# Step 2 of a graph layer: logits behind the group's products, ScalarE's search ahead of their exponentials (slots 1 and 3)

## The chip, the cores and the metric

The kernel runs on one core of one Trainium2 chip. The core has five engines, each with its own queue of instructions, and a wait in a queue holds what stands behind it:

- TensorE (PE in the profile; its weight loads are PEld) multiplies matrices and transposes tiles, out of SBUF into PSUM;
- VectorE (DVE) and ScalarE (ACT) do elementwise work, reductions and exponentials;
- GpSimd (POOL) does elementwise work here and starts the indirect DMAs (gathers);
- SyncE (SP) starts the other DMAs.

The metric is the time of one execution on the device in microseconds. Before the change it was 1398.09 us, the median of three runs (1396.92 to 1398.52).

## What is computed

Two layers over a graph of 2708 nodes with 256 features. Layer 0 is one sparse product, a projection, ReLU and a layer norm. Layer 1 makes two steps of attention that keeps only the largest probabilities of each row up to a mass of 0.9 ("top-p"), beside two products with the normalised graph matrix R. The part that matters here:

```
def _top_p_attention(X, W1, W2, W3):
    q = X @ W1.T @ W2.T
    k = X @ W3.T
    probs = softmax(q @ k.T, axis=-1)
    # keep the largest probabilities of each row until their sum reaches 0.9
    A = probs * mask
    return A / max(A.sum(-1), 1e-12)

for n in range(2):                       # STEPS
    A = _top_p_attention(Xa, W1, W2, W3)
    Xf = R @ Xf
    Xa = A @ Xa
    Z = Z + Xf @ U1[n].T + Xa @ U2[n].T
h = X + Z
out = layernorm(h)                       # then a residual and one more layer norm
```

## The kernel before

**Tiles.** The 2708 rows form NB = 22 blocks of 128 rows (the last has 20). A block of attention is a tile of 128 rows by 2708 columns in SBUF, called e. There are four (e0 to e3), taken in turn; `e2(t)` names the one of block t in step 2. Ahead of step 2 run layer 0, the lists of nonzero chunks of R, and step 1 of the attention. Step 2 starts some 800 us into the span.

**Periods.** Step 2 is the loop `for per in range(NB + 1)` (line 1128). In each period four blocks are in work at once, each one stage further than the next:

- `b_exp`, block per + 2: its logits are computed and exponentiated into e (`logits`, L506; `exps2`, L818, L821 and L822);
- `b_act`, block per + 1: ScalarE searches for the threshold in two rounds (`try_act`): a relu pass over the whole row (L922), a sign pass over the whole row (L925), and steps on single columns (L928, L930, and L935 to L938 in `next_level`);
- `b_dve`, block per: VectorE makes the exact cut (`last_level`, then the generator `finish2`: L976, maxima L979, sorting L576 and L578, marking L1007, and L1010, which writes the masked e);
- `t_mul`, block per - 1: PE transposes e in groups of four 128-column pieces (`turn`: transposes L526 into tr, ScalarE copies tr to wT at L529 and L532) and multiplies the pieces with ya (`products`, L563).

Beside these run the products with R (`r_units`, L730), fed by gathers on GpSimd (`y_load`, L698) and loads on SP, and the layer norms of finished rows (`final_slot`, L1037 to L1077), which need ScalarE's square root and four activations L1047 per period from period 13 on.

**Slots.** A period has NG = 6 slots, one for each group of `turn`. The order is written out by hand: whatever the loop emits first comes first on each engine's queue. `products(1)` in slot g multiplies the group of slot g - 1, so that ScalarE has a slot's time for the copy. The logits of a block come in three parts of 1024, 1024 and 660 columns. Part 0 of the next period's block is emitted in slot 5, and its maximum is taken by VectorE in slot 0 (`shift`, L815) as the shift of the exponentials. Part 1 is computed in slot 1, part 2 in slot 3. The exponentials of the parts are emitted in slots 0, 1 and 3; part 0 has a second one (L822). VectorE sums them in slot 5 (`begin_search`, L826 to L829).

**Buffers.** In PSUM[...] the logits tile `lg` takes two banks and exists once; tr, acc and misc have two of one bank each. So every logits product waits until ScalarE has read the tile for the part before. wT exists twice.

The order inside slots 1 and 3 before, on the queues concerned: PE does the transposes of the group, then (slot 1) the R products and the logits, or (slot 3) the logits and the R products, then the products of the group before. ScalarE does the copy to wT, the exponential of that part, then the search (in both slots: sign pass and small steps).

Of the kernel before, what the change touches and what calls it, by code (L numbers as in the profile page):

```python
# [148 lines left out]
def fast_path(ctx, tc, c, flags, fint, xT_d, x_d, w0_d, b0_d, w1_d, w2_d, w3_d, u1_d, u2_d, g_d, b_d):  # L149
# [13 lines left out]
    def ps_lg():  # L163
        return ps.tile([P, 2, CH], FP, tag="lg", name="lg", bufs=1)
# [4 lines left out]
    def ps_acc(t=None):  # L169
        acc = ps.tile([P, CH], FP, tag="acc", name="acc")  # L170
        if t == NB - 1:
            nc.vector.memset(acc[:, :D + 1], 0.0)
        return acc
# [121 lines left out]
    class Lists:  # L295
# [11 lines left out]
        def turn(self):  # L307
            n = self.n
            parts = names[:, self.a:self.b, :].rearrange("p m (s j) -> p (m s) j", j=3)
            tr = ps_tr()  # L310
            for j in range(3):
                nc.tensor.transpose(tr[:n, j, :], parts[:, :, j], ident)
            nc.scalar.copy(self.row[:n].rearrange("q (j p) -> q j p", j=3), tr[:n, :3, :])
# [184 lines left out]
    def logits(s, t, i):  # L498


        p = rows(t)
        lg = ps_lg()
        cs = CHS[2 * i:2 * i + 2]
        for h, (a, b) in enumerate(cs):
            o = slice(DA * h, DA * h + DA)
            nc.tensor.matmul(lg[:p, h, :b - a], lhsT=q[o, t * P:t * P + p], rhs=keys[s][o, i, :b - a],  # L506
                             start=True, stop=True)
        a, b = cs[0][0], cs[-1][1]
        return lg.rearrange("p h n -> p (h n)")[:p, :b - a], a, b
# [25 lines left out]
    def edge_product(y, acc, e):  # L535

        p = rows(EDGE)
        tr = ps_tr().rearrange("p k i -> p (k i)")[:, :NB * p].rearrange("p (k i) -> p k i", i=p)
        wT = work.tile([P, 4, P], FP, tag="wT", name="wT")
        wT = wT.rearrange("p k i -> p (k i)")[:, :NB * p].rearrange("p (k i) -> p k i", i=p)  # L540
        for k in [NB - 1] + list(range(NB - 1)):
            kw = rows(k)
            nc.tensor.transpose(tr[:kw, k, :], e[:p, k * P:k * P + kw], ident[:p, :p])
        for a, b, kw in ((0, NB - 1, P), (NB - 1, NB, rows(NB - 1))):
            nc.scalar.copy(wT[:kw, a:b, :], tr[:kw, a:b, :])
        for k in range(NB):
            kw = rows(k)
            o = EW * (k % 4)
            nc.tensor.matmul(acc[o:o + p, :D], lhsT=wT[:kw, k, :], rhs=y[:kw, k, :],
                             start=k < 4, stop=k >= NB - 4)  # L550

    def products(keep):

        if len(before) > keep:
            p, ks, wT, y, acc = before.pop(0)
            for k in ks:
                kw = rows(k)
                if p < P:
                    o = EW * (k % 4)
                    nc.tensor.matmul(acc[o:o + p, :D], lhsT=wT[:kw, k % 4, :p], rhs=y[:kw, k, :],  # L560
                                     start=k < 4, stop=k >= NB - 4)
                    continue
                nc.tensor.matmul(acc[:p, :D], lhsT=wT[:kw, k % 4, :p], rhs=y[:kw, k, :],  # L563
                                 start=k == 0, stop=k == NB - 1)
# [153 lines left out]
    def r_units(n):  # L718
        for _ in range(n):
            s, m = r_queue[0]  # L720
            p = rows(m)
            if not r_now:
                r_now[:] = [ps_misc(), 0]
                if m + 1 < NB:
                    r_load(s, m + 1)
            acc, k = r_now
            a, y = r_in[s, m]
            kw = CW if k < CC else p
            rhs = v[:p, m, :] if s and k == CC else y[:kw, k, :]
            nc.tensor.matmul(acc[:p, :D], lhsT=a[:kw, k, :p], rhs=rhs, start=k == 0, stop=k == CC)  # L730
            r_now[1] += 1
            if k == CC:
                r_now.clear()
                r_queue.pop(0)
                r_in.pop((s, m))
                base = za_load(m) if s else None
                later[1].append(lambda s=s, m=m, acc=acc, base=base: r_out(s, m, acc, base))
# [44 lines left out]
    def e2(t):  # L782
        return es[(t + 2) % 4]
# [30 lines left out]
    def shift(b, lg):  # L814
        nc.vector.tensor_reduce(b.nmax, lg[:, :P], AX.X, ALU.max, negate=True)  # L815

    def exps2(b, i, lg, a, c_):
        nc.scalar.activation(e2(b.t)[:b.p, a:c_], lg, AF.Exp, bias=b.nmax, scale=1.0,  # L818
                             accum_out=b.all[:b.p, i:i + 1])
        if i == 0:  # L820
            nc.scalar.activation(b.half, b.nmax, AF.Identity, bias=part_of[:b.p], scale=0.5)  # L821
            nc.scalar.activation(e2(b.t)[:b.p, HC:2 * HC], lg, AF.Exp, bias=b.half, scale=0.5, accum_out=b.roots)  # L822
# [41 lines left out]
    for t in range(NB):  # L864
# [6 lines left out]
        for g in range(NG):  # L871
# [5 lines left out]
            if b and g in (0, 2):  # L877
                lg = logits(1, b.t, g // 2)
# [38 lines left out]
    def try_act(b, k, part):  # L917


        e = e2(b.t)[:b.p, :N]  # L920
        if part == 0:
            nc.scalar.activation(scr[:b.p, :N], e, AF.Relu, bias=b.nz, scale=b.l[k], accum_out=b.relu)  # L922
            return
        if part == 1:
            nc.scalar.activation(scr[:b.p, :N], e, AF.Sign, bias=b.nz, scale=b.l[k], accum_out=b.sign)  # L925
            return
        if part == 2:
            nc.scalar.activation(b.n, b.sign, AF.Identity, bias=halfn[:b.p], scale=0.5)  # L928
            return
        nc.scalar.activation(b.u[k], b.relu, AF.Identity, bias=b.n, scale=b.rz)  # L930
        next_level(b, k)

    def next_level(b, k):
        keep, slope, down = STEPS[k]
        nc.scalar.activation(b.kept, b.l[k], AF.Copy, scale=keep + TOP_P * slope, bias=-down)  # L935
        nc.scalar.activation((b.l1, b.l2)[k], b.u[k], AF.Identity, bias=b.kept, scale=-slope)
        if k:
            nc.scalar.activation(b.few, b.l1, AF.Copy, scale=TOP_P, bias=-FEW)  # L938
# [185 lines left out]
    lg = logits(1, 3, 0)  # L1124
# [3 lines left out]
    for per in range(NB + 1):  # L1128
        if per == NB:
            tail.append(True)  # L1130
        n_r = units.get(per, 0)
        b_act = blocks.get(per + 1)
        b_dve = blocks.get(per)
        t_mul = per - 1 if per else None
        if per:
            accs[t_mul] = ps_acc(t_mul)
        masks = None
        b_exp = None
        if per and per + 2 < NB:
            b_exp = blocks[per + 2] = Block(per + 2)  # L1140
        for g in range(NG):
            n = n_r * (g + 1) // NG - n_r * g // NG
            now = later.pop(0)
            later.append([])
            if g == 0:
                if b_exp:
                    shift(b_exp, lg[0])
                r_units(n)
            if t_mul == EDGE:
                if g == 0:  # L1150
                    products(0)
                    edge_product(ya, accs[EDGE], e2(EDGE))
            elif per:
                turn(t_mul, g, ya, accs[t_mul], e2(t_mul))
            if b_exp and g == 3:
                lg = logits(1, b_exp.t, 2)
            if g == NG - 1 and 3 < per + 3 < NB:
                lg = logits(1, per + 3, 0)
            if g:
                r_units(n)  # L1160
            if b_exp and g == 1:
                lg = logits(1, b_exp.t, 1)
            if t_mul != EDGE:
                products(1 if per else 0)
            if b_exp and g in (0, 1, 3):
                exps2(b_exp, (g + 1) // 2, *lg)
            if b_act:
                for k, part in {0: ((0, 0),), 1: ((0, 1), (0, 2), (0, 3)), 2: ((1, 0),), 3: ((1, 1), (1, 2), (1, 3))}.get(g, ()):
                    try_act(b_act, k, part)
            if g == 0:  # L1170
                if b_dve:
                    last_level(b_dve)
                    masks = finish2(b_dve)
                    next(masks)
                final_slot(0)
                if per > 1:

                    t = t_mul - 1
                    base = za_load(t)
                    later[0].append(lambda t=t, base=base: arrive(t, base, accs.pop(t), ras.pop(t)[:rows(t)]))  # L1180
            elif masks:
                next(masks, None)
                if b_exp and g == 5:
                    begin_search(b_exp)
            for f in now:
                f()
            if g and (per < NB or g < NG - 1):
                final_slot(g)
# [407 lines left out]
```

## Time and profile before

| what | value |
|---|---|
| median of three runs | 1398.09 us |
| the profiled execution: its time, its span | 1400.2 us, 1398.4 us |
| mean granted TensorE clock in it | 0.965 |
| PE busy (matmuls) | 1280.4 us, 92% of the span |
| DVE busy | 1047.2 us, 75% |
| ACT busy | 742.1 us, 53% |
| POOL busy | 639.9 us, 46% |
| starts of L976, one a period, 0 to 21 | 805.16 to 1351.39 us |

Times of instructions are microseconds from the start of the span. A period is counted from one start of L976 to the next. The shares of busy time are means over the whole kernel; layer 0, step 1 and step 2 lean on different engines, so what holds for step 2 must be read from its own stretch. Matmuls are pipelined and the ends of their records are modelled, so that PE's busy time is not PE at its peak.

### The profile page before, as it was taken

The page shows a single profiled execution, that of the slowest core. Times are in us where ns is not written, and L with a number is a line of the kernel's source. Part 1 is how long each engine was busy: PE and PEld are TensorE (multiplying, and loading weights), DVE is VectorE, ACT ScalarE, POOL GpSimd, SP SyncE. Part 2 cuts the span into 40 slices and gives each one's busy share as a digit, 9 for nine tenths or more (in the row PEclk, how much of TensorE's full clock was granted, in tenths as well). Part 3 has the DMA queues.
Part 4 walks back from the last instruction along what each step waited for, and adds up shares of the span by engine and source line. Part 5 has one row for each costly group of instructions (what it writes and reads, how often), then busy time and mean ns, then how long its engine had stood idle before and what let it go on. Part 6 is the DMA issues. An engine that isn't in the chain of part 4 may idle for free.

```text
span 1398.4 us, 18915 instructions
## 1 busy us (share of the span) xinstructions
PE 1280.4 (92%) x5788; PEld 896.5 (64%) x5788; DVE 1047.2 (75%) x3488; ACT 742.1 (53%) x1336; POOL 639.9 (46%) x591
## 2 busy tenths in 40 slices
PE   8999999988999999999998948999998999798884
PEld 6877877833566666666666436777665666566662
DVE  2544545865888887776751279999999989999997
ACT  1000000025455555555554338888787888899950
POOL 1000000013554533775554276777733757767870
PEclk9999999999999999999999779999999999999997
DMA  6544544512222110232123244445432444445441
GB/s 182 179 152 152 164 146 155 162 34 66 65 93 67 50 55 9 88 100 69 58 67 91 71 144 142 145 147 158 147 109 84 132 161 126 132 129 169 136 144 38
DMA packets 92829, 157.93 MB, mean 113 GB/s; under 512 B 16356, under 2 KB 65196, under 8 KB 92720
## 3 DMA queue, kind: packets, MB, share of 16 engines
q1 hardware_dynamic: 66434, 100.59, 22.5%
q0 software_dynamic: 20544, 51.17, 13.0%
q10 hardware_dynamic: 5742, 4.89, 1.2%
q8 instruction: 48, 0.79, 0.2%
q14 instruction: 61, 0.50, 0.1%
HBM read 125.33 MB, written 31.26 MB: 112 GB/s over the span
## 4 chain that ended last, share of the span: by engine, by line
PE 55%; DVE 33%; ACT 5%; issue 2%; another core or an unknown queue 2%; DMA 2%; POOL 0%; ACTq 0%; DVEq 0%; POOLq 0%
PE acc L563 17%; PE acc L255 15%; PE lg L506 6%; DVE cand L979 5%; DVE w L1007 5%; PE tr L526 4%; DVE e L1010 4%; DVE w L976 4%; PE misc L677 3%; DVE srt L576 3%; DVE spare L578 3%; PE acc L649 2%; PE misc L427 2%; PE acc L461 2%
## 5 line engine op out<-in xcount | busy, mean ns | idle before, releaser
L529 ACT COPY wT<-tr 128x512 f32<-128x512 f32 (+2 forms) x258 | 132.3, 518 | 240.1 <-PE tr L526 145.3
L563 PE MATMUL acc<-ya,wT 128*128 128x256 f32 (+1 forms) x924 | 234.3, 393 | 13.4 <-ACT wT L529 8.2
L563 PE MATMUL acc<-x,wT 128*128 128x256 f32 (+1 forms) x924 | 232.8, 391 | 6.0 <-ACT wT L529 5.9
L698 POOL DMA_INDIRECT yg<-yf_d,ix x154 | 191.6, 1244 | 101.7 <-PE misc L730 51.2
L698 POOL DMA_INDIRECT yg<-v_d,ix x154 | 192.6, 1250 | 86.2 <-PE tr L526 38.7
L563 PEld LDWEIGHTS acc<-x,wT 128*128 128x128 f32 (+1 forms) x924 | 166.2, 191 | 87.8 <-issue 50.4
L563 PEld LDWEIGHTS acc<-ya,wT 128*128 128x128 f32 (+1 forms) x924 | 171.1, 193 | 70.1 <-issue 25.1
L255 PE MATMUL acc<-y,adj_t 128*128 128x257 f32 (+1 forms) x924 | 208.8, 382 | 0.0
L365 POOL DMA_INDIRECT adj_t<-in_adj,ix x154 | 170.9, 1110 | 51.0 <-issue 39.6
L255 PEld LDWEIGHTS acc<-y,adj_t 128*128 128x128 f32 (+1 forms) x924 | 171.5, 189 | 34.0 <-issue 10.3
L730 PE MATMUL misc<-yg,adj_t 128*128 128x256 f32 (+1 forms) x660 | 174.5, 398 | 11.8 <-DVE v L753 5.7
L506 PE MATMUL lg<-k,q 64*128 64x512 f32 (+3 forms) x528 | 154.6, 609 | 31.4 <-ACT e L822 28.6
L526 PE MATMUL tr<-ident,e 128*128 128x128 f32 (+2 forms) x946 | 148.4, 276 | 17.7 <-DVE e L1010 17.7
L730 PEld LDWEIGHTS misc<-yg,adj_t 128*128 128x128 f32 (+1 forms) x660 | 118.9, 193 | 59.1 <-issue 20.9
L526 PEld LDWEIGHTS tr<-ident,e 128*128 128x128 f32 (+2 forms) x946 | 113.5, 140 | 60.1 <-issue 16.7
L332 POOL DMA_DIRECT2D part_d<-e x1 | 0.6, 576 | 294.9 <-DVE e L331 294.9
L569 DVE MAX8 cand<-e 128x8 f32<-128x170 f32 (+1 forms) x352 | 88.1, 320 | 39.9 <-ACT e L513 22.4
L922 ACT ACTIVATE w<-e,st 128x2708 f32<-128x2708 f32 (+1 forms) x43 | 113.5, 2640 | 0.0
L925 ACT ACTIVATE w<-e,st 128x2708 f32<-128x2708 f32 (+1 forms) x42 | 111.0, 2642 | 0.1
L438 ACT COPY x1T<-tr 128x256 f32<-128x256 f32 (+1 forms) x22 | 8.0, 364 | 192.2 <-PE tr L437 192.2
L979 DVE MAX8 cand<-w 128x8 f32<-128x136 f32 (+1 forms) x440 | 93.5, 285 | 0.8
L576 DVE MAX8 srt<-spare 128x8 f32<-128x128 f32 (+3 forms) x264 | 81.4, 308 | 9.1
(230 smaller groups left out, 1794.0 us busy)
## 6 DMA issues: line engine op xcount, KB each, us to landing
adj_t<-in_adj SPq DMA_DIRECT2D x44, 704.0 KB
adj_t<-adjc_d SPq DMA_DIRECT2D x44, 448.0 KB
adjc_d<-adj_t SPq DMA_DIRECT2D x22, 256.0 KB
base<-za_d SPq DMA_DIRECT2D x41, 128.0 KB
adjc_d<-adj_t SPq DMA_DIRECT2D x22, 192.0 KB
xt<-in_x ACTq DMA_DIRECT2D x21, 128.0 KB
x_d<-x SPq DMA_DIRECT2D x21, 128.0 KB
x1b_d<-xb SPq DMA_DIRECT2D x21, 128.0 KB
```

What stands on the lines that cost most here:

```text
L255: nc.tensor.matmul(acc[:p, :n], lhsT=halves[k // KH][:kw, k % KH, :p], rhs=y[:kw, k, :n], start=k == 0, stop=stop and k == NB - 1)
L365: nc.gpsimd.indirect_dma_start(out=a[:CW, i, :], out_offset=None, in_=adj_rows, in_offset=bass.IndirectOffsetOnAxis(ap=ix[:CW, m, i:i + 1] ...
L506: nc.tensor.matmul(lg[:p, h, :b - a], lhsT=q[o, t * P:t * P + p], rhs=keys[s][o, i, :b - a], start=True, stop=True)
L526: nc.tensor.transpose(tr[:kw, k % 4, :p], e[:p, k * P:k * P + kw], ident[:p, :p])
L529: nc.scalar.copy(wT[:, :full, :p], tr[:, :full, :p])
L563: nc.tensor.matmul(acc[:p, :D], lhsT=wT[:kw, k % 4, :p], rhs=y[:kw, k, :], start=k == 0, stop=k == NB - 1)
L576: nc.vector.max(dst[:p, i:i + 8], src[:p])
L698: nc.gpsimd.indirect_dma_start(out=y[:CW, i, :], out_offset=None, in_=rows_d, in_offset=bass.IndirectOffsetOnAxis(ap=ix[:CW, m, i:i + 1], ...
L730: nc.tensor.matmul(acc[:p, :D], lhsT=a[:kw, k, :p], rhs=rhs, start=k == 0, stop=k == CC)
L922: nc.scalar.activation(scr[:b.p, :N], e, AF.Relu, bias=b.nz, scale=b.l[k], accum_out=b.relu)
L925: nc.scalar.activation(scr[:b.p, :N], e, AF.Sign, bias=b.nz, scale=b.l[k], accum_out=b.sign)
L979: nc.vector.max(cand[:p, 8 * i:8 * i + 8], w[:p, SEG2 * i:SEG2 * (i + 1)])
```

## The change

In slots 1 and 3 of the periods that have a block to exponentiate (`b_exp`, periods 1 to 19) the call of `logits` moves behind `products`, and the call of `exps2` moves behind the calls of `try_act`. In slot 0 the exponentials of part 0 stay where they were, ahead of the relu pass. In slot 5 nothing changes.

```diff
             elif per:
                 turn(t_mul, g, ya, accs[t_mul], e2(t_mul))
-            if b_exp and g == 3:
-                lg = logits(1, b_exp.t, 2)
             if g == NG - 1 and 3 < per + 3 < NB:
                 lg = logits(1, per + 3, 0)
             if g:
                 r_units(n)
-            if b_exp and g == 1:
-                lg = logits(1, b_exp.t, 1)
             if t_mul != EDGE:
                 products(1 if per else 0)
-            if b_exp and g in (0, 1, 3):
-                exps2(b_exp, (g + 1) // 2, *lg)
+            if b_exp and g in (1, 3):
+                lg = logits(1, b_exp.t, (g + 1) // 2)
+            if b_exp and g == 0:
+                exps2(b_exp, 0, *lg)
             if b_act:
                 for k, part in {0: ((0, 0),), 1: ((0, 1), (0, 2), (0, 3)), 2: ((1, 0),), 3: ((1, 1), (1, 2), (1, 3))}.get(g, ()):
                     try_act(b_act, k, part)
+            if b_exp and g in (1, 3):
+                exps2(b_exp, (g + 1) // 2, *lg)
             if g == 0:
                 if b_dve:
                     last_level(b_dve)
```

## The prediction

> **What bounds the kernel now.** I read the page first, for the span and the busy shares, then the busy time stretch by stretch, then the timelines of TensorE (PE), ScalarE (ACT) and VectorE (DVE) inside single periods of step 2. The change lies wholly in step 2, which takes the last 590 us.
>
> ```profile
> span 1398.4 us, 18915 instructions
> DVE  2544545865888887776751279999999989999997
> core 0: us, PE busy (x) PEld busy (x) DVE busy (x) ACT busy (x) POOL busy (x), PEclk, DMA share, GB/s
> 985.50:1010.00 24.50, 23.22 (x113) 17.11 (x112) 23.48 (x80) 19.97 (x34) 18.48 (x15) 1.00 0.49 150
> 1162.50:1189.30 26.80, 23.95 (x113) 16.92 (x111) 25.62 (x90) 24.21 (x40) 21.40 (x18) 1.00 0.47 148
> ```
>
> Each stretch is one period, from one start of L976 to the next. DVE is busy 23.48 of 24.5 us, the rest being small gaps between its own instructions, so it sets the pace. But PE has 23.22 us and, in the periods that also finish output rows (13 to 19), ACT has 24.21 of 26.8. Nobody is far behind. Such an engine can be pushed over the edge by a wait alone, so I looked at who waits for whom around the tile of the logits. It exists once, so each product into it waits for ScalarE's last exponential out of it. PE, period 7:
>
> ```profile
> 987.48 1.13 PE L506 MATMUL lg<-k,q 64*128 64x512 f32 x4 [0.32 <-ACT e L822]
> 988.53 1.99 PE L563 MATMUL acc<-ya,wT 128*128 128x256 f32 x8
> ...
> 1001.88 1.13 PE L506 MATMUL lg<-k,q 64*128 64x512 f32 x4
> 1002.93 1.56 PE L730 MATMUL misc<-yg,adj_t 128*128 128x256 f32 x6
> 1004.33 1.89 PE L563 MATMUL acc<-ya,wT 128*128 128x256 f32 x8
> 1006.06 1.03 PE L730 MATMUL misc<-yg,adj_t 128*128 128x256 f32 x4
> 1008.05 0.63 PE L526 MATMUL tr<-ident,e 128*128 128x128 f32 x4 [0.96 <-DVE e L1010]
> ```
>
> Columns: start, length, instruction, and in brackets the idle time before it and what ended it. PE loses 0.32 us before the logits of slot 1; before those of slot 5 (1001.88, for the next block) nothing. It then waits 0.96 us for DVE's L1010 before the next period's first transpose. That 0.96 us is PE's whole slack. ACT, same period:
>
> ```profile
> 984.31 0.59 ACT L529 COPY wT<-tr 128x512 f32<-128x512 f32 x1 [4.16 <-issue]
> ...
> 998.43 0.57 ACT L529 COPY wT<-tr 128x512 f32<-128x512 f32 x1
> 998.90 0.81 ACT L818 ACTIVATE e<-lg,nmax 128x660 f32<-128x660 f32 x1
> 999.60 0.20 ACT L818 ACTIVATION_READ_ACCUMULATOR e<-lg,nmax 128x1 f32 x1
> 999.70 2.64 ACT L925 ACTIVATE w<-e,st 128x2708 f32<-128x2708 f32 x1
> ...
> 1003.50 0.19 ACT L938 ACTIVATE st<-st 128x1 f32<-128x1 f32 x1
> 1003.60 0.73 ACT L529 COPY wT<-tr 128x512 f32<-128x512 f32 x2
> ```
>
> From 984.31 to 1003.60 ACT has no gap. The third exponential (L818, 660 columns, slot 3) ends at 999.71, over 2 us before PE wants the tile at 1001.88. Behind it stands the search: the sign pass L925 and the scalar steps L928 to L938, to 1003.60.
>
> **What the Trainium skill says.** "PSUM — Partial Sum Buffer", section "Engine vs sequencer instructions": the queues of ScalarE, VectorE and GpSimd are strict FIFO, and matmuls start and complete in program order. The trace agrees: in slot 1, PE's products stand idle behind the waiting logits. So a blocked logits product holds all of PE. "Perfetto Trace Analysis", section "Optimization Strategy": the same gap repeating on the engine that should be saturated can mean too few buffers; the 0.32 us gap in period after period, released by the tile's reader, is that. "TensorE: Matmul & The Clock Gate", Part 1, says PE drops to half clock after an idle window of about 3.4 us. Here, behind an idle time of 5.45 us, the logits at 1224.70 took 2.08 us instead of 1.13; this enters a rival.
>
> **The change, part by part.** No instruction is added or removed, no DMA moves; two orders change. One period (numbers of period 7):
>
> 1. PE, slot 1: the products of group 0 pass ahead of the logits. Their wT was copied at 984.31, so they start at once; the logits then come 1.9 us later, past the 0.32 us wait. Gain on PE 0.32 us (1.7 us in periods 14 and 17 to 19, where the table load of 1.28 us delays the exponentials). But next, in slot 2, PE needs ACT's copy of group 1, whose time has not moved: PE has 1.6 us to spare there in period 7, while in period 14 it already waits 0.27 us, so the gain becomes a longer wait. I count 0.
>
> 2. ACT, slot 1: sign pass and scalar steps (3.8 us) ahead of the second exponential, 1.1 us. The next copy comes when it came before. The slot 3 logits are the next to want the tile; the exponential now ends at 995.4 and they stand behind products that wait for that copy (995.32 to 995.9) and last 1.9 us. Cost 0.
>
> 3. PE, slot 3: products first, logits 1.06 us later. The third exponential starts at 1002.8 at the earliest (next point), so it is covered. Cost 0.
>
> 4. ACT, slot 3: the third exponential moves behind the sign pass and steps, from 998.90 to 1002.80, and ends at 1003.61. PE's slot 5 logits follow it: with the 0.15 us that the trace shows from the end of L822 (962.86) to the logits (963.01), they start at 1003.76, not 1001.88. That is **1.88 us later, against 0.96 us of slack**. This is the step that decides. Behind the waiting logits stand, on PE, the R products of slot 5, the products of group 4, those R products of slot 0 and the next first transpose.
>
> So a closed loop appears: ACT's first copy to the end of the third exponential, 1003.61 - 984.31 = 19.3 us; release 0.15; slot 5 logits to the next first transpose when nothing else holds it, 5.05 us (859.59 to 864.64 in period 1); transpose to copy 0.7 us (864.64 to 865.33). Sum **25.2 us**, against DVE's 24.46. In periods 14 to 18 the copy-to-copy part is 22.6 us (1161.29 to 1183.93 in period 14), because of the table load and four norm activations (L1047) in slot 0; loop 28.5 us against DVE's 26.8. Period 13: 21.6 us, loop 27.5. Period 10 has no R products, which fill 1.4 us of that stretch in slot 5 (1002.93 to 1004.33): 23.8.
>
> **When does DVE feel it?** DVE's shift (L815) reads slot 5's logits, and begin_search reads the third exponential. Period 1 shows the shift waiting:
>
> ```profile
> 860.77 0.29 DVE L815 TENSOR_REDUCE nmax<-lg 128x1 f32<-128x128 f32 x1 [0.82 <-PE lg L506]
> ```
>
> There L976 follows at 862.23 and ACT's first copy at 865.33. So L976 can't start earlier than 3.1 us before that copy. In the undisturbed periods the copy is 1.2 us ahead of L976, so the loop may fall 4.3 us behind before DVE pays. Adding up from the copy at 865.1 in period 2: eight loops of 25.2 to period 10 (1066.7), 23.8 to 11 (1090.5), two of 25.2 or 25.3 (1141.0), 27.5 (1168.5), five of 28.5: period 19 at 1311.0. Less 3.1, L976 of period 19 at 1307.9, where it was 1298.82: 9.1 us. By period 10 it is 4.5 us (1063.6 against 1059.14). Some 2.4 us that DVE already loses in periods 15 to 17 (28.54, 27.01 and 27.25 us, against 26.8) are within this sum. Period 19's begin_search could add 1 us. The tail doesn't touch the logits and keeps its length. I take **+9 us**: 1409.2 for a profiled execution, whose time before was 1400.2 (span 1398.4); the median shown, 1398.09, is 2.1 lower, so **1407**. An error of 0.15 us in the loop is 2.6 us over 17 periods: 1402 to 1411 is this case's own range.
>
> **Rivals.**
> - PE at half clock: in the final periods PE stands some 2.6 us before slot 5's logits (period 14: group 3's copy ends at 1179.34, its products and a transpose take 2.0 us, the exponential ends at 1183.93). Should this bring half clock for the 5 us stretch behind it, up to 5 us are added each time, right on the loop. Against: PE stands less elsewhere. Two such periods give 1415; chance 0.18.
> - The other side, not slower: DVE's slack swallows it. Ends of matmuls are modelled, so the 5.05 us stretch may be shorter. With 4.3 us or less the loop is 24.45 us, the light periods lose nothing, and five final ones lose 0.95 each, 4.7 us, about the 4.3 us that the slack takes. It decides from a loop of 24.5 us. 1398.5; chance 0.12. Against: 5.05 us is seen with PE working without a gap.
> - Faster: PE's 1.7 us in slot 1 of the final periods feed R products and gathers sooner and end the 2.4 us of DVE losses: 1395.5; chance 0.07. Against: ACT's copies don't move.
> - The orders come out as before in effect, because something else releases the tile: 1398; chance 0.05.
>
> **How the numbers follow.** The forecast has 0.58. Range 1398.5 to 1414: it takes in the upper part of the second rival and most of the first. 0.2% is 2.8 us, about what a measurement of this kernel tells from no change. Slower 0.58 + 0.18 + 0.02 of the second rival = 0.78; same 0.05 + 0.09 of it = 0.14; faster 0.07 + 0.01 = 0.08.
>
> **What would show it.** Right: PE's idle time before the logits passes from L822 to the third exponential, L818, about 1.2 us in the light periods (PE reaches slot 5 earlier by what it no longer loses) and over 2 in the final ones; no wait on L1010; DVE waiting before L815; L976 starts 25.2 and 28.5 us apart. Wrong: L976 still 24.46 us apart with PE waiting for L1010; or half-clock stretches on PE in the final periods.

## The result, and the profile after the change

The changed kernel takes **1415.51 us** (median of four runs, 1413.86 to 1417.31) against 1398.3 us for the kernel before, run beside it (four runs, 1396.92 to 1405.27). The ratio is 1.0124, with a 95% interval of 1.0099 to 1.015. It is slower, as forecast, but by 17 us where 9 were forecast.

The profiled execution took 1417.31 us. First its page: the span, the row of VectorE's busy tenths, and of the chain that ended last its shares by engine.

```profile
span 1415.5 us, 18896 instructions
...
DVE  2554545876888877767741569999997999989996
...
PE 66%; ACT 21%; DVE 9%; issue 2%; another core or an unknown queue 1%; DMA 0%; POOL 0%; ACTq 0%; DVEq 0%; POOLq 0%
```

The same line of the kernel before:

```profile
PE 55%; DVE 33%; ACT 5%; issue 2%; another core or an unknown queue 2%; DMA 2%; POOL 0%; ACTq 0%; DVEq 0%; POOLq 0%
```

This is the shortest sign that the bound has changed. Before, a third of the chain ran over VectorE. Now it has 9%, and the share has gone to PE and ACT. The busy times have hardly moved (PE 1284.0 us against 1280.4, DVE 1049.4 against 1047.2): no engine got more work, so the time went into waits.

Now single periods (each from one start of L976 to the next): period 8, the undisturbed pace of the light periods, then periods 10, 17 and 18.

```profile
core 0: us, PE busy (x) PEld busy (x) DVE busy (x) ACT busy (x) POOL busy (x), PEclk, DMA share, GB/s
1013.88:1039.05 25.17, 23.17 (x112) 17.03 (x111) 23.62 (x80) 19.92 (x33) 17.23 (x15) 1.00 0.49 144
1064.22:1094.06 29.84, 22.61 (x95) 15.80 (x95) 23.36 (x79) 20.15 (x33) 16.07 (x15) 0.89 0.35 107
1256.98:1285.51 28.53, 23.48 (x112) 16.93 (x111) 26.10 (x89) 24.86 (x40) 19.08 (x18) 1.00 0.42 134
1285.51:1314.36 28.85, 25.50 (x114) 18.30 (x113) 26.07 (x89) 24.86 (x40) 20.35 (x19) 0.94 0.45 139
```

25.17 and 28.53 us a period are the two lengths of the closed loop that the prediction worked out (25.2 and 28.5). DVE is now busy 23.62 of 25.17 us, so it waits.

The loop can be followed through period 8. TensorE, from slot 3 on (start, length, instruction, idle time before it and what ended it):

```profile
1028.68 1.99 PE L563 MATMUL acc<-ya,wT 128*128 128x256 f32 x8 [1.09 <-ACT wT L529]
1030.60 1.12 PE L506 MATMUL lg<-k,q 64*128 64x512 f32 x4
...
1036.47 1.13 PE L506 MATMUL lg<-k,q 64*128 64x512 f32 x4 [0.91 <-ACT e L818]
...
1041.52 0.60 PE L526 MATMUL tr<-ident,e 128*128 128x128 f32 x4
```

ScalarE:

```profile
1017.04 0.59 ACT L529 COPY wT<-tr 128x512 f32<-128x512 f32 x1 [5.02 <-PE tr L526]
...
1035.53 0.79 ACT L818 ACTIVATE e<-lg,nmax 128x660 f32<-128x660 f32 x1
...
1042.21 0.59 ACT L529 COPY wT<-tr 128x512 f32<-128x512 f32 x1 [5.02 <-PE tr L526]
```

VectorE:

```profile
1037.64 0.29 DVE L815 TENSOR_REDUCE nmax<-lg 128x1 f32<-128x128 f32 x1 [0.54 <-PE lg L506]
...
1039.05 3.05 DVE L976 SCALAR_TENSOR_TENSOR w<-e,st 128x2720 f32<-128x2720 f32 x1
```

From the first copy (1017.04) to the end of the third exponential (1036.32) are 19.28 us, to slot 5's logits 0.15, to the next first transpose (1041.52) 5.05, to the next first copy 0.69: 25.17 us. PE's wait for L1010 is gone; it stands before slot 5's logits instead, released by the third exponential L818. DVE waits 0.54 us for these logits before L815. In period 17 the same four parts are 22.67, 0.14, 5.05 and 0.69 us, 28.55 in all.

Where the 17.1 us between the two spans lie, from the starts of L976:

| stretch | before | after | difference |
|---|---|---|---|
| ahead of step 2, its period 0, and the tail | 884.22 | 888.56 | +4.3 |
| periods 1 to 9 | 221.93 | 223.55 | +1.6 |
| period 10 | 24.27 | 29.84 | +5.6 |
| periods 11 to 18 | 215.41 | 220.30 | +4.9 |
| periods 19 and 20 | 52.57 | 53.25 | +0.7 |

The first row is work that the change doesn't touch. In the profiles of all the kernels below, the start of step 2 alone differs by up to 6 us on one chip, also between kernels whose code is the same up to there; nothing here explains it, and no reading below rests on it. More than half of the growth of periods 10 to 18 lies in period 10; it gets a part of its own below.

### The profile page after: what moved, and what is told of

The parts are those of the page before. It is cut to its first block, busy times and chain, and to the rows that moved or that the text cites. A ratio compares the mean times of both kernels' runs of the same rounds, so it can differ in the third digit from the quotient of the medians.

```text
span 1415.5 us, 18896 instructions
## 1 busy us (share of the span) xinstructions
PE 1284.0 (91%) x5788; PEld 898.4 (63%) x5788; DVE 1049.4 (74%) x3488; ACT 742.4 (52%) x1336; POOL 639.0 (45%) x591
## 3 DMA queue, kind: packets, MB, share of 16 engines
q0 software_dynamic: 20544, 51.17, 12.8%
## 4 chain that ended last, share of the span: by engine, by line
PE 66%; ACT 21%; DVE 9%; issue 2%; another core or an unknown queue 1%; DMA 0%; POOL 0%; ACTq 0%; DVEq 0%; POOLq 0%
PE acc L563 20%; PE acc L255 15%; PE lg L506 8%; PE tr L526 5%; PE misc L730 5%; ACT w L922 5%; ACT w L925 4%; PE misc L677 3%; ACT e L818 3%; ACT wT L529 2%; PE acc L649 2%; PE misc L427 2%; PE acc L461 2%; PE misc L422 2%; PE misc L390 2%
## 5 line engine op out<-in xcount | busy, mean ns | idle before, releaser
L563 PE MATMUL acc<-ya,wT 128*128 128x256 f32 (+1 forms) x924 | 238.1, 399 | 39.0 <-ACT wT L529 32.3
L698 POOL DMA_INDIRECT yg<-yf_d,ix x154 | 196.1, 1274 | 106.2 <-PE misc L730 52.0
L563 PEld LDWEIGHTS acc<-ya,wT 128*128 128x128 f32 (+1 forms) x924 | 175.4, 197 | 83.3 <-ACT wT L529 42.0
L698 POOL DMA_INDIRECT yg<-v_d,ix x154 | 186.5, 1211 | 86.5 <-PE tr L526 32.3
L506 PE MATMUL lg<-k,q 64*128 64x512 f32 (+3 forms) x528 | 151.4, 601 | 25.1 <-ACT e L818 14.5
```

Source lines behind the costliest of these rows:

```text
L698: nc.gpsimd.indirect_dma_start(out=y[:CW, i, :], out_offset=None, in_=rows_d, in_offset=bass.IndirectOffsetOnAxis(ap=ix[:CW, m, i:i + 1], ...
```

## The experiments

Twelve kernels ran in three groups, each group on one chip and beside the kernel before. There the kernel before took 1396.05, 1371.49 and 1371.19 us (the first, second and third chip below). Absolute times in the expectations start from a kernel before of some 1398 us; they are to be read as differences from the kernel before, and only ratios compare groups. A ratio stands here as it was recorded with its interval; it is not the quotient of the two medians and can differ from it (the order on TensorE alone: 1.0036 recorded, 1.0054 from the medians). Four kernels (named "filled") add matrix products with a tile of zeros to the sums, which leaves the sums as they are.

### One edit alone, and the change without it

The third exponential alone moved behind the search, PE's order as before:

```diff
-            if b_exp and g in (0, 1, 3):
+            if b_exp and g in (0, 1):
                 exps2(b_exp, (g + 1) // 2, *lg)
             if b_act:
...
+            if b_exp and g == 3:
+                exps2(b_exp, 2, *lg)
```

> The kernel before with one edit: in slot 3 the third exponential goes behind the search; slot 1 and the order on PE stay. Theory L (the loop from ScalarE's first copy over the third exponential to slot 5's logits, 25.2 us in light periods and 28.5 us in final ones): all of the loss comes back, 1412 to 1417 us, L976 25.1 to 25.2 us apart in periods 7 to 9, VectorE idle before L815. Rival S (slot 1's moves or PE's new order carry a good part): under 1407 us.

Measured: 1413.2 us, ratio 1.0146 (1.0112 to 1.0181). One edit gives the whole loss. Of the light periods 2 to 9 all but one took 25.06 to 25.19 us. PE in this kernel:

```profile
1003.57 1.13 PE L506 MATMUL lg<-k,q 64*128 64x512 f32 x4 [1.81 <-ACT e L818]
1004.63 2.68 PE L730 MATMUL misc<-yg,adj_t 128*128 128x256 f32 x6
```

With PE's old order its idle time lies in one piece, 1.81 us, before slot 5's logits, where the changed kernel has 0.91 there and 1.09 in slot 3. The loop is as long either way. The R products behind it took 2.68 us, not 1.56: a stretch of half clock, treated below. The period that follows took 26.86 us instead of 25.18.

The changed kernel with the third exponential alone back ahead of the search:

```diff
-            if b_exp and g == 0:
-                exps2(b_exp, 0, *lg)
+            if b_exp and g in (0, 3):
+                exps2(b_exp, (g + 1) // 2, *lg)
...
-            if b_exp and g in (1, 3):
-                exps2(b_exp, (g + 1) // 2, *lg)
+            if b_exp and g == 1:
+                exps2(b_exp, 1, *lg)
```

> The changed kernel with one edit: in slot 3 the third exponential goes ahead of the search again; all other moves stay. Theory L: 1396 to 1401 us, L976 24.5 us apart in periods 6 to 9, PE idle before L1010's release again and not before slot 5's logits. Rival S: more than 1404 us.

Measured: 1400.66 us, ratio 1.0038 (1.0022 to 1.0055). Four of the light periods 2 to 9 are back at 24.44 or 24.45 us (the longest took 25.12), and slot 5's logits follow their transpose with no wait. Some 0.4% remain, which the loop doesn't explain.

### An attempt to cut the loop

Slot 5's logits moved behind the R products and the products of group 4, so that these no longer wait for the third exponential in PE's queue:

```diff
-            if g == NG - 1 and 3 < per + 3 < NB:
-                lg = logits(1, per + 3, 0)
             if g:
                 r_units(n)
             if t_mul != EDGE:
                 products(1 if per else 0)
+            if g == NG - 1 and 3 < per + 3 < NB:
+                lg = logits(1, per + 3, 0)
```

> The changed kernel with one edit: slot 5's logits go behind the R products and the products of group 4, so that nothing of slot 5 but the logits waits for the third exponential. Theory L: the loop is cut (about 22 us in light periods, 25.5 in final ones), 1396 to 1402 us, with the third exponential as late as in the changed kernel. Rival S: as the changed kernel, 1412 to 1417 us.

Measured: 1409.29 us, ratio 1.0099 (1.0067 to 1.0131). The light periods came down to 24.54 us, but the final ones, 14 to 18, took 27.9 to 30.8, the longest three at a clock of 0.89 (two of them) and 0.94. That lies between the theory and the rival, nearer to the rival. The same cut with PE's old order in slots 1 and 3, and both exponentials late, on the second chip:

```diff
+            if b_exp and g == 3:
+                lg = logits(1, b_exp.t, 2)
...
+            if b_exp and g == 1:
+                lg = logits(1, b_exp.t, 1)
             if t_mul != EDGE:
                 products(1 if per else 0)
-            if b_exp and g in (1, 3):
-                lg = logits(1, b_exp.t, (g + 1) // 2)
+            if g == NG - 1 and 3 < per + 3 < NB:
+                lg = logits(1, per + 3, 0)
```

> Both exponentials behind the search as in the changed kernel, but the logits of slots 1 and 3 ahead of the products as before, and slot 5's logits behind the products. Theory L with O: light periods 24.5 us, and in the final ones less loss than the 13 us of the kernel that kept the new order on PE: 1396 to 1403 us. Rival: the third exponential's lateness costs in the final periods by another way than slot 5's chain: still 1406 us or more.

Measured: 1382.05 us, ratio 1.0078 (1.0052 to 1.0104). Final periods 27.05 to 29.49 us; 10.6 us over the kernel before is the rival's size (8 or more), not the theory's. And the cut of the first of these two with zero products against the half clock (light periods two in slot 3; period 10 four in slot 2 and eight in slot 3; periods 13 on four in each), on the third chip:

```diff
+            if g in (2, 3) and 0 < per < NB - 1:
+                fill(per, g)
             if t_mul != EDGE:
                 products(1 if per else 0)
```

> The changed kernel with slot 5's logits behind the products (loop cut), and with zero products ahead of the products of slots 2 and 3 (period 10: 4 and 8; final: 4 and 4; light: 2 in slot 3). Theory: with loop and clock both mended the third exponential's lateness costs nothing, 0 to 3 us over before. Rival (the late exponential costs by a third way): 8 us or more over before.

Measured: 1374.77 us, ratio 1.0023 (1.0013 to 1.0033). The theory had 0 to 3 us over before; the medians give 3.6, the interval 1.8 to 4.5. Here the clock is full in periods 2 to 19, so the remaining loss can be read. ScalarE and then TensorE at the end of period 16:

```profile
1211.92 0.79 ACT L818 ACTIVATE e<-lg,nmax 128x660 f32<-128x660 f32 x1
...
1212.70 0.73 ACT L529 COPY wT<-tr 128x512 f32<-128x512 f32 x2
...
1217.97 0.58 ACT L529 COPY wT<-tr 128x512 f32<-128x512 f32 x1 [2.79 <-PE tr L526]
```

```profile
1213.33 2.00 PE L563 MATMUL acc<-ya,wT 128*128 128x256 f32 x8
1215.25 1.13 PE L506 MATMUL lg<-k,q 64*128 64x512 f32 x4
1216.31 1.13 PE L730 MATMUL misc<-yg,adj_t 128*128 128x256 f32 x4
1217.28 0.60 PE L526 MATMUL tr<-ident,e 128*128 128x128 f32 x4
```

The first copy of that period began at 1190.05, the next at 1217.97: 27.92 us, the length of the period. The loop closes by another way. Group 4's copy to wT stands behind the third exponential on ACT too, so the products that were to go first wait for the same engine; the logits and the next transpose come after them. The cost of a final period falls from 1.7 to 1.1 us, no further. So with the clock full the cut takes away most of the loss: 1.0129 is left with slot 5's logits ahead (the filled kernel further below), 1.0023 with them behind. This is a second test of the loop, made on PE and not on ScalarE. The rest stays as long as the exponential stands behind the search. In the two kernels without zero products much of that gain is missing; their final periods have clocks of 0.89 to 1.00.

### Period 10

In the profile of the changed kernel period 10, which has no R products, took 29.84 us, where 24.27 stood before. PE and then DVE there:

```profile
1078.36 1.99 PE L563 MATMUL acc<-ya,wT 128*128 128x256 f32 x8 [2.94 <-ACT wT L529]
...
1086.16 1.26 PE L506 MATMUL lg<-k,q 64*128 64x512 f32 x4 [2.22 <-ACT e L818]
1088.16 3.78 PE L563 MATMUL acc<-ya,wT 128*128 128x256 f32 x8 [0.74 <-issue]
```

```profile
1092.65 0.29 DVE L815 TENSOR_REDUCE nmax<-lg 128x1 f32<-128x128 f32 x1 [4.86 <-PE acc L563]
```

PE stood 2.94 and 2.22 us, the products behind ran at half speed (3.78 us for 1.99), and L815 waited 4.86 us. A mean clock of 0.89 over 29.84 us accounts for at most 3.3 of the 5.6 us; where the others come from is not shown. The changed kernel with the third exponential ahead of the search in this one period:

```diff
-            if b_exp and g == 0:
-                exps2(b_exp, 0, *lg)
+            if b_exp and (g == 0 or g == 3 and per == 10):
+                exps2(b_exp, (g + 1) // 2, *lg)
...
-            if b_exp and g in (1, 3):
+            if b_exp and (g == 1 or g == 3 and not (per == 10)):
```

> The changed kernel, but in period 10 alone the third exponential of slot 3 goes ahead of the search. Theory P (period 10, which took 29.84 us instead of 24.27, loses some 5 us by PE standing idle there and running at half clock behind it): 1409 to 1412 us, period 10 under 26 us. Rival N (those 5 us are chance of one execution): 1413 to 1417 us. Theory L alone, with period 10 as forecast, says a gain of at most 1.5 us.

Measured: 1408.9 us, ratio 1.0104 (1.0062 to 1.0145). Period 10 took 24.26 us, but the interval overlaps that of the changed kernel, and in the profiles of the kernel with the third exponential alone and of the changed kernel on the third chip (below) period 10 took 24.5 us in both. So 29.84 us isn't a fixed part of the change. How often it occurs stays open.

### The order on TensorE alone, and the waits that it uncovers

Logits behind the products in slots 1 and 3, both exponentials ahead of the search as before the change (second chip):

```diff
-            if b_exp and g == 3:
-                lg = logits(1, b_exp.t, 2)
...
-            if b_exp and g == 1:
-                lg = logits(1, b_exp.t, 1)
             if t_mul != EDGE:
                 products(1 if per else 0)
+            if b_exp and g in (1, 3):
+                lg = logits(1, b_exp.t, (g + 1) // 2)
```

> The changed kernel's order on PE alone: the logits of slots 1 and 3 behind the products, both exponentials ahead of the search as before. Theory O (the order on PE costs by itself in the periods with norms: PE waits some 2 us for wT before the products of slots 2 and 3, with no logits to fill it, and a half-clock spell follows in each such period): 4 to 9 us over before, a spell in most periods from 13 on, light periods at 24.5 us. Rival A (what the kernel with only the third exponential ahead lost comes from the second exponential behind the search of slot 1): within 2 us of before.

Measured: 1378.93 us, ratio 1.0036 (1.0019 to 1.0054): a loss of its own. The light periods are undisturbed (24.44 to 24.46). In final period 16 PE shows this in slots 2 and 3:

```profile
1205.53 3.33 PE L563 MATMUL acc<-ya,wT 128*128 128x256 f32 x8 [2.05 <-ACT wT L529]
1208.65 0.99 PE L526 MATMUL tr<-ident,e 128*128 128x128 f32 x4
1209.48 1.03 PE L730 MATMUL misc<-yg,adj_t 128*128 128x256 f32 x4
1210.90 1.99 PE L563 MATMUL acc<-ya,wT 128*128 128x256 f32 x8 [0.39 <-ACT wT L529]
```

Eight product records took 3.33 us and four transposes 0.99, where 1.99 and 0.60 are usual: half clock, after a wait of 2.05 us for the copy. Before the change the logits that now stand behind filled such waits. To test whether the half clock is the loss, the kernel without the third exponential's move (ratio 1.0038 above) got four zero products ahead of the products in slots 2 and 3 of periods 13 to 20:

```diff
+    none = small.tile([P, P], FP, tag="none", name="none", bufs=1)
+    nc.gpsimd.memset(none, 0.0)
+    def fill(n):
+        for _ in range(n):
+            nc.tensor.matmul(accs[t_mul][:, :D], lhsT=none, rhs=ya[:, 0, :], start=False, stop=False)
...
+            if 13 <= per < NB - 1 and g in (2, 3):
+                fill(4)
             if t_mul != EDGE:
                 products(1 if per else 0)
```

> The changed kernel with the third exponential ahead of the search, and in periods 13 to 20, slots 2 and 3, four products with a tile of zeros (0.9 us, added to the same sums, so that the result stays) ahead of the products that wait for wT. It adds work and takes away idle time. Theory H (the half-clock spells after these waits make the loss of the final periods): fewer spells and 3 to 6 us less than the 1400.7 us without them, 1395 to 1398 us. Rival (the waits themselves, not the clock): the same or up to 3 us more.

Measured: 1371.92 us, ratio 1.0005 (0.9991 to 1.0019): level with the kernel before. The comparison crosses chips: without zero products this kernel ran on the first one, and its nearest neighbour on the second, PE's order alone with 1.0036, has the second exponential ahead too. The four products took 1.89 us, not 0.9: each makes two records. The same place of period 16, TensorE:

```profile
1195.43 1.89 PE L1111 MATMUL acc<-ya,none 128*128 128x256 f32 x8
1197.64 1.99 PE L563 MATMUL acc<-ya,wT 128*128 128x256 f32 x8 [0.32 <-ACT wT L529]
```

Final periods of the kernel with PE's order alone, then of the filled one:

```profile
1193.54:1220.57 27.03, 24.59 (x109) 17.73 (x108) 25.85 (x90) 24.45 (x40) 20.59 (x18) 0.94 0.47 147
1220.57:1248.12 27.55, 25.11 (x111) 18.07 (x111) 25.89 (x89) 24.95 (x41) 20.58 (x19) 0.94 0.47 144
```

```profile
1187.71:1214.48 26.77, 26.09 (x123) 19.30 (x122) 25.59 (x89) 24.96 (x40) 20.20 (x18) 1.00 0.46 143
1214.48:1241.38 26.90, 26.23 (x125) 19.41 (x124) 25.72 (x89) 24.96 (x40) 20.48 (x18) 1.00 0.47 147
```

The granted clock (the column of 0.94 and 1.00) is the difference: more work on PE and less time. 26.8 us is VectorE's own pace in these periods.

### The loop in one part of step 2

The kernel before, with the third exponential late in periods 1 to 11 alone:

```diff
-            if b_exp and g in (0, 1, 3):
+            if b_exp and (g in (0, 1) or g == 3 and per >= 12):
                 exps2(b_exp, (g + 1) // 2, *lg)
...
+            if b_exp and g == 3 and per < 12:
+                exps2(b_exp, 2, *lg)
```

> The kernel before, with the third exponential behind the search in periods 1 to 11 only. Theory L as summed in the prediction: 4 to 5 us over before (eight loops of 25.2 us, less what the loop may fall behind before VectorE pays), L976 25.2 us apart from period 7 on, the periods from 12 on as before. If light periods pay from the first: 7 us or more.

Measured: 1378.62 us, ratio 1.0047 (1.0026 to 1.0068), that is 3.6 to 9.3 us over before, which doesn't decide between 4 to 5 and 7. L976 was 25.17 us apart from period 5 on, not 7; a period of 26.86 us ahead of it had used up the slack. Three of its periods: light ones without and with a stretch of half clock, and final period 15, which runs in the order of before.

```profile
938.46:963.63 25.17, 23.06 (x112) 17.22 (x111) 23.63 (x80) 19.93 (x33) 18.08 (x15) 1.00 0.50 147
988.80:1015.66 26.86, 24.75 (x114) 18.45 (x113) 23.64 (x79) 19.93 (x33) 17.80 (x15) 0.95 0.47 136
1168.75:1195.56 26.81, 23.95 (x112) 16.97 (x110) 25.62 (x90) 25.02 (x41) 20.98 (x18) 1.00 0.49 148
```

The last row is the important one. In the first profile of the kernel before, periods 12 and 15 to 17 took 27.35, 28.54, 27.01 and 27.25 us. Here, with the same order, they took 25.54 and 26.80 to 26.82. So those were disturbances of that execution or of its chip, not VectorE's pace. With five zero products ahead of slot 5's logits in periods 1 to 11 (third chip):

```diff
+            if g == NG - 1 and 0 < per < NB - 1:
+                fill(per, g)
             if g == NG - 1 and 3 < per + 3 < NB:
                 lg = logits(1, per + 3, 0)
```

> The kernel before with the third exponential late in periods 1 to 11, and five zero products ahead of slot 5's logits there. Theory: without the two or three spells of the light periods the loop alone is left, 4 to 5 us over before, L976 25.2 us apart from period 6 or 7 on and none of 26.8. Rival (VectorE's slack is smaller than 4.3 us): 7 us as without the zero products.

Measured: 1376.76 us, ratio 1.0049 (1.0032 to 1.0065). No period of 26.86 is left, but the periods are now 25.46 apart: the five zero products themselves delay the logits by 0.3 us in each. So the two cancel, and this run tells nothing of what the half clock costs. Its periods 12 to 18 took 25.51 and 26.77 to 27.06 us, which gives VectorE's pace a second time.

### The loop, or the half clock behind it?

The changed kernel once more, on the third chip, with no edit, beside one with zero products ahead of the places where its PE waits (light periods two each in slots 3 and 5; period 10 four, eight and six in slots 2, 3 and 5; periods 13 on four, four and three):

```diff
+            if g == NG - 1 and 0 < per < NB - 1:
+                fill(per, g)
             if g == NG - 1 and 3 < per + 3 < NB:
                 lg = logits(1, per + 3, 0)
             if g:
                 r_units(n)
+            if g in (2, 3) and 0 < per < NB - 1:
+                fill(per, g)
```

> The changed kernel itself, on the chip of the three kernels beside it. Loop and clock together: 1.2 to 1.3% over before (16 to 18 us).

> The changed kernel, with products by a tile of zeros put where PE stands idle: ahead of slot 3's products and slot 5's logits in the light periods (2 each), ahead of the products of slots 2 and 3 and slot 5's logits in period 10 (4, 8, 6) and in the final ones (4, 4, 3). The loop is as long as before, the clock stays full. Theory: what is left over before is the loop alone, as the prediction summed it, 8 to 11 us; period 10 under 26 us, no spell of half clock from period 2 to 19. Rival (the loop alone makes the whole 17 us): within 3 us of the changed kernel.

Measured: 1389.73 us, ratio 1.0141 (1.0117 to 1.0166), without the filling, and 1388.38, ratio 1.0129 (1.0105 to 1.0152), with it. Two final periods without it, then one with it:

```profile
1171.28:1199.82 28.54, 25.19 (x112) 18.13 (x111) 26.07 (x89) 24.85 (x40) 20.16 (x18) 0.94 0.43 135
1199.82:1229.02 29.20, 25.07 (x112) 17.81 (x111) 26.08 (x89) 24.97 (x40) 20.57 (x19) 0.94 0.44 140
```

```profile
1169.09:1197.96 28.87, 28.19 (x134) 21.06 (x133) 26.08 (x90) 24.86 (x40) 20.36 (x19) 1.00 0.45 137
```

With the clock full the periods are still 28.87 us long, 0.3 of it from the three zero products of slot 5. I had expected the filling to win back a good part; that fell. The loop makes nearly the whole loss. The half clock is in all of these final periods without the filling, and lengthens every second of them by 0.65 us (29.20 against 28.54), some 2 us in all. In the others it costs nothing: in period 15 it comes after the wait for the copy in slot 2, and the wait in slot 3 then shrinks from 2.08 to 0.40 us, which takes it up; in period 16 it comes after the wait in slot 3, and only the 0.91 us ahead of slot 5's logits are left to take up a part.

### All runs

| kernel | ratio to the kernel before | light period, undisturbed | final periods 14 to 18 |
|---|---|---|---|
| changed | 1.0124 | 25.17 | 28.5 to 29.0 |
| third exponential late, alone | 1.0146 | 25.18 | 28.2 to 30.2 |
| changed, third exponential ahead | 1.0038 | 24.45 | 26.9 to 30.8 |
| changed, slot 5 logits late | 1.0099 | 24.54 | 27.9 to 30.8 |
| changed, period 10 ahead | 1.0104 | 25.16 | 28.5 to 30.7 |
| PE order alone | 1.0036 | 24.45 | 26.8 to 27.6 |
| old PE order, slot 5 logits late | 1.0078 | 24.45 | 27.1 to 29.5 |
| third exponential ahead, filled | 1.0005 | 24.45 | 26.8 to 26.9 |
| third exponential late until 11 | 1.0047 | 25.17 | 26.8 to 27.1 |
| changed, again | 1.0141 | 25.17 | 28.5 to 29.2 |
| changed, filled | 1.0129 | 25.17 | 28.8 to 28.9 |
| slot 5 logits late, filled | 1.0023 | 24.54 | 26.8 to 27.9 |
| late until 11, filled | 1.0049 | 25.46 | 26.8 to 27.1 |

No version beats the kernel before; the filled one with 1.0005 can't be told from it.

## Why the forecast had the cause right and the size wrong

**Points 1 and 3, the order on PE ("I count 0", "Cost 0").** Right only in company with point 4. By itself this order costs 0.36% (0.19 to 0.54), because PE has nothing left to do in slots 2 and 3 of a final period before the copies come, and waits some 2 us. Point 1 saw its wait coming, as "a longer wait" for wT; in slot 3 none was named. What neither priced is the half clock behind these waits. In the changed kernel on the third chip it costs some 2 us; PE there waits for the loop anyway.

**Point 2, ScalarE in slot 1 (cost 0).** Right as far as the runs show: the kernel with the second exponential behind the search and the third ahead lost as much (1.0038, first chip) as the one with both ahead (1.0036, second chip). No kernel moved the second exponential alone.

**Point 4, the third exponential.** Right: alone it gives the whole loss, without it 0.4% remain, and the loop's four terms are within 0.2 us of the forecast (19.28, 0.15, 5.05 and 0.69 us in period 8). The next L976 began 3.16 us ahead of the next first copy (3.1 forecast). PE's wait for slot 5's logits was 0.91 and 0.92 us in the undisturbed periods of both kinds (8 and 17), where 1.2 and over 2 had been forecast, since the rest of its idle time lies before the copies.

**The sum: this is the step that failed.** It followed ScalarE's first copy from loop to loop, period 10 to 19, in 244.3 us (1066.7 to 1311.0). The changed kernel on the third chip took 245.72 from L976 to L976. So the loop's own side was right to 1.4 us. The term that failed is what was subtracted: 239.68 us, the periods 10 to 18 of the one profile shown, taken as VectorE's pace. It held a period 12 of 27.35 us and "2.4 us that DVE already loses in periods 15 to 17", and these losses were taken to be "within this sum". VectorE's undisturbed pace over the stretch is 235.16 us (third exponential ahead, filled) or 235.69 (late until 11, filled). Forecast 4.6 us, measured 10.0 to 10.6. No profile of the kernel before was taken on these chips; that it runs at this pace there is inferred from the ratio of 1.0005 of the first of these kernels, and from periods 12 to 18 of the second, which run in the order of before.

In the profiled pair of the result the same 10.5 us come about by another way, and that the two agree so closely is luck. There the sum held for periods 11 to 18: 4.9 us where 5.1 were summed, so in these periods the losses of before did vanish under the loop. The surplus is period 10, summed at 23.8 us, 0.5 less than before, and measured at 29.84, 5.6 more. Half clock in period 10 was not among the rivals, which looked for it in the final periods. The kernels with the third exponential alone and with period 10 ahead have a period 10 of 24.5 and 24.3 us, but 248.87 and 249.27 us in the stretch, since their final periods are longer. So all these profiles carry some 3 to 4.5 us above the undisturbed lengths, the kernel before as well as the changed ones, and the difference between them stays. Why the chips of these profiles show more of it than the other two is not known.

In periods 1 to 9 it went the other way: 4.5 us forecast, 1.6 measured in the first pair of profiles, and 3.2 on the other chips (223.11 us against 219.92). The forecast began from a period 2 whose first copy already stood 2.9 us behind L976 (865.1; the trace has 865.33, 3.1 us behind). In the changed kernel's profile it stood 1.2 us behind, so some 1.9 us of slack had to be used up first.

**Left out.** Period 19 was put beside the sum as "could add 1 us" and then not added; it took 0.7 us more (27.27 against 26.60).

**The rivals.** Half clock on PE came, as that rival said, but not at its price: up to 5 us each were put down. Measured in the final periods of the changed kernel and of the one with period 10 ahead were nothing (28.54 us at a clock of 0.94), 0.65, and at most 2.2 us (period 18 of the latter: 30.72 us at 0.89). Its total of 1415 agrees with the result by accident: with the clock full the loss is still 1.29%. That slack swallows the delay was excluded by the light periods at 25.17 us; that the kernel gets faster or stays level, by the result itself.

The median difference of the result is 17.2 us, of which the profiled pair has 12.8 in periods 1 to 20 and 4.3 elsewhere; the kernel with the third exponential alone has 16.9 in those periods (531.10 against 514.18). On the third chip the changed kernel has 14.6 in them (522.51 us against 507.93 of the filled kernel that is level with before), and its median is 18.5 above. About 4 us of that are not accounted for; they lie outside these periods, and the start of step 2, which moves without a reason that I found, is one candidate, which was not tested.

## What to carry to other kernels

Where several engines are loaded nearly alike, moving an instruction behind others on a queue is to be priced as a closed loop: from the moved instruction to whoever waits for it, across the boundary of the period, back to its own engine, and compared with the bounding engine's period. That engine's pace is to be taken from undisturbed periods, not from the sum of one profile that holds losses of its own, since these differ from execution to execution and chip to chip. And when an engine slows down after idling, work that fills one of its waits is worth more than its length: once it is moved away, the wait that it leaves costs its own length and a slow stretch behind it.

## What the runs showed of the hardware

**Half clock after short waits.** The Trainium skill, "TensorE: Matmul & The Clock Gate", section "HAM oscillation — how this bites in real kernels", puts the danger at idle gaps of PE over some 3.4 us. Here one wait of about 2 us was enough in a PE that is busy for more than 80% of the time: in the kernel with the order on TensorE alone (1205.53, above) no other wait stood within 9 us ahead of it. In period 16 of the changed kernel on the third chip it came behind the second of two:

```profile
1212.62 1.99 PE L563 MATMUL acc<-ya,wT 128*128 128x256 f32 x8 [2.05 <-ACT wT L529]
...
1217.99 3.22 PE L563 MATMUL acc<-ya,wT 128*128 128x256 f32 x8 [2.08 <-ACT wT L529]
1221.15 1.54 PE L506 MATMUL lg<-k,q 64*128 64x512 f32 x4
```

A mean clock of 0.94 over 28.54 us is a loss of 1.7 us, that is some 3.4 us at half speed, which is the length of the page's window. But the same two waits (2.04 and 2.08 us) stand in period 17 of the first profile, whose clock was 1.00: such a wait is not sufficient. In the light periods single waits of 1.8 us were followed by it now and then (26.86 us instead of 25.17, the same 1.7 us).

More can be seen when periods are cut in stretches of 3.41 us along the times at which the granted clock changes; in every profile all these times lie on one grid of that step. First the kernel with the order on TensorE alone around 1205.53, then the changed kernel in its undisturbed period 17 (columns as above; the busy time of PE comes first, the granted clock follows that of POOL):

```profile
1202.60:1206.00 3.40, 1.35 (x7) 0.87 (x6) 3.09 (x14) 3.40 (x8) 1.32 (x2) 1.00 0.36 116
1206.00:1209.40 3.40, 3.40 (x12) 2.71 (x11) 3.13 (x15) 3.37 (x5) 2.87 (x5) 0.50 0.51 128
```

```profile
1267.90:1271.35 3.45, 1.59 (x7) 1.44 (x8) 3.04 (x13) 3.45 (x5) 2.37 (x4) 1.00 0.35 114
1271.35:1274.75 3.40, 1.70 (x10) 1.15 (x8) 2.61 (x13) 3.30 (x9) 2.65 (x4) 1.00 0.62 199
```

Counted over periods 2 to 19 of all fourteen profiles, by PE's records (transposes counted as work) and from full clock: behind a stretch of the grid in which PE idles for less than 40% half clock never follows (0 of 1703), behind one with 60% and more always (40 of 40), in between in 29 of 91. A wait of 2 us is 60% of a stretch if it falls wholly into one, and less if the grid cuts it. This is a count, and no run shifted a wait along the grid to test it.

**Work that saves time.** Four products with a tile of zeros (eight records, 1.89 us) ahead of each of the two waits bring the clock to 1.00 in periods 13 to 20 and the ratio from 1.0038 on the first chip to 1.0005 on the second.

**Groups of runs differ.** The kernel before took 1398 and 1396 us beside the changed kernel and in the first group, and 1371 us in the other two groups. In the profiles period 0 of step 2 took 31.2 to 34.1 us in the former and 23.9 to 24.0 in the latter, with the same code. The three groups ran on three chips; that the chip is the cause was not tested.
